# Two block plans in turn, and layer 0's maxima on another engine, in a fused two-layer graph-attention kernel

## The chip, the core and the metric

The kernel runs on one core of a Trainium2 chip. The core has five engines, each with a queue of its own that is worked off in order: TensorE (PE: matrix products into PSUM; its weight loads are PEld), VectorE (DVE), ScalarE (ACT), GpSimd (POOL, which does not read PSUM here) and SyncE (SP, which issues nearly all DMAs of this kernel). The metric is the device time of one execution in microseconds (us).

## The reference

Two layers over a graph of 3327 nodes with 128 features; `adj` is 3327 x 3327, 0 or 1, with ones on the diagonal.

```python
# layer 0: x = layernorm(x + gat(x, adj))
Hm = X @ W.T + b;  s = Hm @ a_s;  r = Hm @ a_r
e = leaky_relu(A * s + A * r.T, 0.2)
att = softmax(where(A > 0, e, NEG), axis=1);  out = att @ Hm
# layer 1: x = layernorm(x + graphormer(x, adj, adj)), H = 8
q, k, v = ((x @ Wq.T).reshape(d, n, h), ...)
a = einsum('dnh,dmh->dnm', q, k) * d ** -0.5
a = softmax(a + adj + adj, axis=2)
out = einsum('dnm,dmh->dnh', a, v).reshape(n, h * d) @ Wo.T
```

Layer 1 is the work: for each of the 128 features a full 3327 x 3327 attention with head size 8.

## The kernel before, in words

**Tiles.** The features are taken in 32 *groups* of 4. The 3327 queries are cut into 7 *blocks* of 476 (the last 472), so there are 224 blocks. The 3327 keys are 26 *chunks* of 128 or 127. For a block and a chunk the kernel needs scores (keys x queries) for 4 features, the exponential of twice (score/2 + adj), and the product with the values, which is summed over the 26 chunks in one PSUM tile `av`.

**Scores** (`pair_scores`, L154): two matmuls of one pair of features make one PSUM tile `scb` of 2 x 476 columns. A chunk has two halves (h = 0, 1), one for each pair.

**Two ways to bring in the adjacency.** Most chunks: VectorE adds `adj` to the PSUM scores and writes SBUF (L1139), half by half, and ScalarE later takes the exponential in SBUF (`exp_late`, L968), a whole chunk of 1904 columns at a time. GpSimd's chunks (`times`: 0, 3, ..., 24): ScalarE takes the exponential straight out of PSUM (L1136), and GpSimd multiplies by a factor that is 1 or e squared (L1137). The factor is made from `adj` by GpSimd (`make_factor`, L782) the first time and kept in DRAM (`ftd`). In what follows P is an exponential out of PSUM (952 columns), S a whole one in SBUF (1904 columns).

**Rounds.** A block is 26 *rounds* of two halves. Of three chunks i, i+1, i+2 the rounds are A: (i, half 1) and (i+1, half 0); B: (i, half 0) and (i+1, half 1); C: both halves of i+2. So A and B have one add and one P each, C two adds. Each round issues in this order: the loads of a coming stretch, the four score matmuls, the P and its multiplication or the adds, the S that have fallen due (`late`, normally the round after the chunk's last add), the products of the chunk that stands four rounds back (`products`, L938; LAG = 4), and side work. Chunks 24 and 25 are the last two rounds (A and B alone). Chunk 23's and chunk 25's exponentials are not done whole: `late` lists their halves one by one, chunk 23's in the last two rounds, chunk 25's in the first two rounds of the next block.

**Buffers.** `scb` has one PSUM tile for the chunks of `times` (pool `pe`) and two for the others (pool `pd`); `av` has one: the first products of a block wait until VectorE has copied the block before out of it (`o4`, L948, issued just behind the last products, which come in the fourth round of the next block). The exponentials have 7 tiles (`e4`), the loaded adjacency 5 (`at`, one for each *stretch* of three chunks; `want_adj` asks for it AHEAD = 3 stretches early). Side work has one PSUM tile (`bank`).

**Side work.** Layer 0 for rows of 128 queries, the projections to q, k, v that follow it, and the output projection of finished rows run in the gaps. They are lists of units: kind "p" for TensorE, "d" for VectorE, "m" for GpSimd, "x" for DMAs. `lane` says in which rounds a unit may be issued (mostly the B rounds), `work_tensor` and `work` issue them. Layer 0's weights are `weigh` (a maximum of a row and a scalar, L310, 650 of them on VectorE) and `mask` (times `adj`, GpSimd, L319). A projection is cut in columns of 128 (`QW`): `project` (TensorE), then `halves` on VectorE: the rounded value `hi` (L405) and the remainder `lo` (L408). `finish_to` forces what is not done when the keys of the next group are loaded. `judge` tests at the end that the shortcuts were valid for the data (if not, a slower general program runs, which is not the case here).

Of the kernel before, what the change touches and what calls it, by code (L numbers as in the profile page):

```python
# [8 lines left out]
F32 = mybir.dt.float32  # L9
# [8 lines left out]
P = 128  # L18
# [29 lines left out]
def kernel(  # L48
# [70 lines left out]
    NTR = NT // 3  # L119
    NP = NTR + (NT % 3 == 2)  # L120
    times = {3 * j for j in range(NP)}
    stretch = [list(range(i, min(i + 3, NT))) for i in range(0, NT, 3)]
    NST = len(stretch)
    where = {i: (i % 3 if NT % 3 != 1 or i < NT - 1 else 1) for i in range(NT)}
    assert all(kr[i] == P for i in times)
# [26 lines left out]
    def special():  # L152
# [9 lines left out]
        with ExitStack() as sx, tc.manual_schedule(engines=ALL):  # L162
# [106 lines left out]
            def layer0(t, side=True, trow=None, bank=bank, held=None):  # L269
# [31 lines left out]
                def weigh(n, c0, c1):  # L301
# [3 lines left out]
                    for i in range(c0, c1):  # L305
                        w, e = s["w"][n][:, i - i0, :r], er[:, i : i + 1]
                        if side:

                            w = s["w"][n][:, i - i0, :].rearrange("p (a b) -> p a b", b=T3)
                            nc.vector.tensor_scalar(w, s["t"][:, :, :T3], e, None, op0=ALU.max)  # L310
# [79 lines left out]
                QW = 128 if side else 512  # L390
# [7 lines left out]
                def halves(dst, c, scale):  # L398
# [3 lines left out]
                    o = c % 512  # L402
                    hi, lo = s["hi"], s["lo"]
                    if side:
                        nc.vector.tensor_scalar(hi[:r, o : o + QW], s["b"][:r, :QW], scale, None, op0=ALU.mult)  # L405
                    else:
                        nc.scalar.mul(hi[:r, o : o + QW], s["b"][:r, :QW], scale)
                    nc.vector.scalar_tensor_tensor(  # L408
# [34 lines left out]
                for w, dst, sc in ((wk, kT, 1.0), (wq, qT, half_scale)):  # L443
                    for c in range(0, H * D, QW):
                        chain += [
                            ("p", lambda w=w, c=c: project(w, c)),
                            ("d", lambda dst=dst, c=c, sc=sc: halves(dst, c, sc)),
# [15 lines left out]
                for n, (i0, i1) in enumerate(CH):  # L463

                    aside.append(("n", ("P", q0 + n - 2, 0)))
                    for c0 in range(i0, i1, 3):
                        c1 = min(c0 + 3, i1)
                        aside.append(("d", lambda n=n, c0=c0, c1=min(c0 + 2, c1): weigh(n, c0, c1)))
                        if c0 + 2 < c1:
                            aside.append(("d", lambda n=n, c0=c0 + 2, c1=c1: weigh(n, c0, c1)))  # L470
                        if side:
                            aside.append(("m", lambda n=n, c0=c0, c1=c1: mask(n, c0, c1)))
# [269 lines left out]
            stretches = [(g, b, m) for g in range(NG) for b in range(NBLK) for m in range(NST)]  # L742
            adjs = {}
            RAW = max(NBLK, AHEAD + 3) * NST

            def want_adj(n):
# [6 lines left out]
                cs = stretch[m]  # L753
                if n >= RAW and cs[0] in times:
                    nc.sync.dma_start(a[:, 0, :w], ftd[b][m][:, :w])
                    cs = cs[1:]
                for of in [cs[:-2], cs[-2:]] if len(cs) > 2 else [cs]:
                    if not of:
                        continue
                    z = where[of[0]]  # L760
# [16 lines left out]
            def make_factor(n):  # L777
                if n < min(RAW, len(stretches)) and stretch[stretches[n][2]][0] in times:
                    g, b, m = stretches[n]
                    w = exact[b][2]  # L780
                    f = adjs[n][:, 0, :w]
                    nc.gpsimd.tensor_scalar(f, f, E2 - 1.0, 1.0, op0=ALU.mult, op1=ALU.add)  # L782
                    if g == 0:
                        issue(lambda: nc.sync.dma_start(ftd[b][m][:, :w], f))
# [132 lines left out]
            rounds, order, starts = [], [], {}  # L917
            for m, st_ in enumerate(stretch):
                starts[len(rounds)] = m
                if len(st_) > 1:  # L920
                    i = st_[0]
                    rounds += [[(i, 1), (i + 1, 0)], [(i, 0), (i + 1, 1)]]
                    order += [i + 1, i]
                for i in st_[2:] if len(st_) > 1 else st_:
                    rounds.append([(i, 0), (i, 1)])
                    order.append(i)
            NR = len(rounds)
# [56 lines left out]
            def lane(kind, n):  # L984
                middle = n % 3 == 1 and 4 <= n < NR - 2
# [558 lines left out]
```

## Time and profile before

| what | value |
|---|---|
| median of three runs | 10001.89 us (9998.2 to 10005.2) |
| profiled execution | 10004.91 us |
| its span (first to last instruction) | 10003.1 us |
| granted TensorE clock | 0.996 |
| P: L1136 on ScalarE | 4032, mean 1012 ns |
| S and halves: L968 on ScalarE | 4256, mean 1678 ns |
| adds: L1139 on VectorE | 7616, mean 1143 ns |
| multiplications: L1137 on GpSimd | 4032, mean 2237 ns |
| DMA | 1728.31 MB, mean 173 GB/s |

Busy time is the union of an engine's instructions; their mean durations can overlap, so the time that one more instruction costs is read from start to start. A row of a group has count, busy us, mean ns of one, then the idle time before them and what ended it. A row of a timeline has the start (us from the span's start), the duration, engine, line, operation, tiles, shape and count; in brackets the idle time of the engine before it and what ended that.

### The profile page before, as it was taken

How to read it: one execution, taken by the hardware profiler on the slowest of the kernel's cores; microseconds unless marked ns; L12 is line 12 of the kernel's file. 1: busy time of each engine (PE TensorE's matmuls, PEld its weight loads, DVE VectorE, ACT ScalarE, POOL GpSimd, SP SyncE). 2: the span in 40 equal slices, each digit the busy share in tenths (PEclk: the TensorE clock that was granted, in tenths of full speed). 3: DMA queues.
4: the chain of work that ended last, by engine and by line, in shares of the span. 5: the costliest groups of instructions: out<-in, count | busy, mean ns of one | idle time of the engine just before them, and what ended most of it. 6: DMA issues, size and time to landing. Idle time of an engine off the chain costs nothing.

```text
span 10003.1 us, 212173 instructions
## 1 busy us (share of the span) xinstructions
PE 9461.4 (95%) x81923; PEld 3078.5 (31%) x81923; DVE 9334.1 (93%) x11592; ACT 9892.4 (99%) x8352; POOL 9201.7 (92%) x4416
## 2 busy tenths in 40 slices
PE   7999999999999999999999999999999999999998
PEld 2233333333233333323333332333332333332222
DVE  7999999999999999999999999999999999999998
ACT  7999999999999999999999999999999999999998
POOL 7999999999999999999999999999999999999998
PEclk9999999999999999999999999999999999999999
DMA  7665666655656656656566665566665566656554
GB/s 200 200 176 169 177 172 177 178 167 174 177 165 175 182 161 178 177 169 176 165 173 174 181 179 164 163 178 179 177 174 168 164 179 177 175 161 171 167 168 125
DMA packets 1383200, 1728.31 MB, mean 173 GB/s; under 512 B 347463, under 2 KB 1370657, under 8 KB 1378079
## 3 DMA queue, kind: packets, MB, share of 16 engines
q1 hardware_dynamic: 1371828, 1712.03, 60.1%
q8 instruction: 644, 10.55, 0.4%
q10 hardware_dynamic: 10347, 2.61, 0.1%
q14 instruction: 381, 3.12, 0.1%
HBM read 1610.23 MB, written 103.93 MB: 171 GB/s over the span
## 4 chain that ended last, share of the span: by engine, by line
ACT 40%; PE 24%; POOL 16%; issue 11%; DVE 6%; DMA 2%; SPq 1%; POOLq 0%; ACTq 0%; DVEq 0%
ACT e L968 25%; POOL e L1137 16%; ACT e L1136 15%; PE scb L154 12%; PE av L938 11%; DVE e L1139 4%; PE bank L243 1%; DVE o L948 1%; DVE lo L408 0%; DMA q4b<-qT 0%; POOL w L319 0%; DMA at<-ftd 0%; DVE hi L405 0%; DMA k4b<-kT 0%; DVE w L310 0%
## 5 line engine op out<-in xcount | busy, mean ns | idle before, releaser
L1137 POOL TENSOR_TENSOR e<-e,at 128x952 f32<-128x952 f32 (+1 forms) x4032 | 8956.7, 2237 | 718.9 <-ACT e L1136 641.7
L1139 DVE TENSOR_TENSOR e<-scb,at 128x952 f32<-128x952 f32 (+1 forms) x7616 | 8420.0, 1143 | 579.3 <-PE scb L154 477.8
L968 ACT ACTIVATE e<-e 128x1904 f32<-128x1904 f32 (+2 forms) x4256 | 7104.0, 1678 | 2.0 <-DVE e L1139 1.6
L938 PE MATMUL av<-e,v4b 128*32 128x476 f32 x46592 | 5917.6, 572 | 60.6 <-DVE o L948 41.9
L154 PE MATMUL scb<-q4b,k4b 32*128 32x476 f32 (+1 forms) x23296 | 3749.2, 486 | 442.8 <-ACT e L1136 370.8
L1136 ACT ACTIVATE e<-scb 128x952 f32<-128x952 f32 (+1 forms) x4032 | 4078.6, 1012 | 57.5 <-PE scb L154 33.8
L154 PEld LDWEIGHTS scb<-q4b,k4b 32*128 32x128 f32 (+1 forms) x23296 | 1764.2, 189 | 5371.8 <-ACT e L1136 3489.9
L938 PEld LDWEIGHTS av<-e,v4b 128*32 128x32 f32 x46592 | 1059.2, 108 | 1140.0 <-issue 933.0
L243 PE MATMUL bank<-hsb,w 128*32 128x129 f32 (+1 forms) x5200 | 277.8, 285 | 0.0
L328 DVE TENSOR_SCALAR_CACHE_REDUCE dump<-a 128x384 bf16<-128x384 f32 (+2 forms) x468 | 247.1, 528 | 0.6
L319 POOL TENSOR_TENSOR w<-w,a 128x384 f32<-128x384 f32 (+3 forms) x225 | 207.7, 923 | 0.1
L310 DVE TENSOR_SCALAR w<-trow,er 128x129 f32<-128x129 f32 x650 | 201.1, 338 | 0.0
L948 DVE COPY o<-av 128x476 f32<-128x476 f32 (+1 forms) x224 | 145.9, 651 | 8.1 <-PE av L938 7.2
L243 PEld LDWEIGHTS bank<-hsb,w 128*32 128x32 f32 (+1 forms) x5200 | 102.4, 108 | 148.0 <-issue 148.0
L408 DVE SCALAR_TENSOR_TENSOR lo<-bank,hi 128x128 fp32r<-128x128 f32 (+1 forms) x400 | 116.5, 291 | 13.8
L405 DVE TENSOR_SCALAR hi<-bank 128x128 fp32r<-128x128 f32 (+1 forms) x400 | 112.0, 280 | 0.0
L243 PE MATMUL bank<-wv,x1T 128*32 128x128 f32 x1600 | 85.6, 286 | 3.9 <-DVE vb L429 3.9
L243 PE MATMUL bank<-wq,x1T 128*32 128x128 f32 x1600 | 85.4, 285 | 0.0
L243 PE MATMUL bank<-wk,x1T 128*32 128x128 f32 x1600 | 85.4, 285 | 0.0
L243 PE MATMUL bank<-wo,ot 128*32 128x128 f32 x1600 | 85.2, 285 | 0.0
L429 DVE COPY vb<-bank 128x128 f32<-128x128 f32 (+1 forms) x200 | 56.1, 281 | 5.8 <-PE bank L243 5.8
L503 PE MATMUL bank<-ident,o 128*128 128x128 f32 x225 | 52.0, 304 | 0.0
(123 smaller groups left out, 659.7 us busy)
## 6 DMA issues: line engine op xcount, KB each, us to landing
at<-in_adjT_dram SPq DMA_DIRECT2D x1536, 476.0 KB
at<-ftd SPq DMA_DIRECT2D x1674, 238.0 KB
at<-in_adjT_dram SPq DMA_DIRECT2D x256, 472.0 KB
at<-ftd SPq DMA_DIRECT2D x279, 236.0 KB
k4b<-kT SPq DMA_DIRECT2D x128, 415.9 KB
q4b<-qT SPq DMA_DIRECT2D x1528, 29.8 KB
at<-in_adjT_dram SPq DMA_DIRECT2D x186, 208.2 KB
a<-in_adjT_dram SPq DMA_DIRECT2D x50, 504.0 KB
```

The source lines that it names most:

```text
L154: nc.tensor.matmul(dst, k4[32 * j : 32 * j + H4, first_key(i) : first_key(i) + 2 * r - 1 : 2], q4[32 * j : 32 * j + H4, :nb], start=True, ...
L243: nc.tensor.matmul(dst[c0:c1], w[:, c0:c1], mov, **kw)
L310: nc.vector.tensor_scalar(w, s["t"][:, :, :T3], e, None, op0=ALU.max)
L319: nc.gpsimd.tensor_tensor(w, w, s["a"][n][:, c0 - i0 : c1 - i0, :r], op=ALU.mult)
L328: nc.vector.tensor_scalar(z, a, float(k), None, op0=ALU.is_equal, op1=ALU.add, accum_out=even[:, t, at : at + 1])
L408: nc.vector.scalar_tensor_tensor(lo[:r, o : o + QW], s["b"][:r, :QW], scale, hi[:r, o : o + QW].bitcast(F32), op0=ALU.mult, op1=ALU.subtract,)
L938: nc.tensor.matmul(s.av[32 * j : 32 * j + 32, : s.w], s.v4[:r, j, i * H1 : i * H1 + 32], e[:r, j, : s.w], start=(s.left == NT - 1), stop=( ...
L948: nc.vector.tensor_copy(o4[:, :w], s.av[:, :w])
L968: nc.scalar.activation(e, e, AF.Exp, scale=2.0)
L1136: nc.scalar.activation(eh, z[:r, :, :w], AF.Exp, scale=2.0)
L1137: nc.gpsimd.tensor_tensor(eh, eh, ah, op=ALU.mult)
L1139: nc.vector.tensor_tensor(eh, z[:r, :, :w], ah, op=ALU.add)
```

## The change

- **Two plans in turn.** Even blocks (counted over the whole run) keep 9 chunks for GpSimd. An odd block starts with a round of chunk 25 alone (two adds), goes on with the eight triples, and ends with one round of chunk 24 alone: its half 1 goes the GpSimd way, its half 0 is added by VectorE. So an odd block has 17 P and 35 adds in place of 18 and 34. It has ten stretches in place of nine, and chunk 24 needs both its factor and its plain adjacency there.
- **Exponentials whole.** `late` no longer splits chunks 23 and 25; all are due one round after the last add. The one half left is chunk 24's in odd blocks.
- **Maxima on GpSimd.** `weigh` becomes a GpSimd `tensor_scalar` (minimum with 3e38, then maximum), three to a unit of kind "m", and `mask` is a unit of its own.
- **Projections of 256 columns** in place of 128, and `halves` becomes `high` (kind "d") and `low` (kind "l"), which is issued a round after.
- **Other places for side work.** `lane` depends on the plan: in odd blocks all places are one round later, and "m" units, which had one in any round, now go only where "d" units may. Even: rounds 4, 7, ..., 22, 0 and 25; odd: 5, 8, ..., 23 and 25; "l" one round after each. "p" has also the round 3 (odd: 4).
- **Factors.** `made_by` holds the stretch that makes a block's factor, since the two plans number their stretches differently.

```diff
+    threes = [(i, [i + 1, i + 2]) for i in range(0, NT - 2, 3)]
+    plans = [threes + [(NT - 2, [NT - 1])], [(None, [NT - 1])] + threes + [(NT - 2, [NT - 2])]]
...
-                            nc.vector.tensor_scalar(w, s["t"][:, :, :T3], e, None, op0=ALU.max)
+                            nc.gpsimd.tensor_scalar(w, s["t"][:, :, :T3], -LOWEST, e, op0=ALU.min, op1=ALU.max)
...
-                QW = 128 if side else 512
+                QW = 256 if side else 512
...
-                            ("d", lambda dst=dst, c=c, sc=sc: halves(dst, c, sc)),
+                            ("d", lambda c=c, sc=sc: high(c, sc)),
+                            ("l", lambda dst=dst, c=c, sc=sc: low(dst, c, sc)),
...
-                        aside.append(("d", lambda n=n, c0=c0, c1=min(c0 + 2, c1): weigh(n, c0, c1)))
-                        if c0 + 2 < c1:
-                            aside.append(("d", lambda n=n, c0=c0 + 2, c1=c1: weigh(n, c0, c1)))
-                        if side:
-                            aside.append(("m", lambda n=n, c0=c0, c1=c1: mask(n, c0, c1)))
+                        aside.append(("m", lambda n=n, c0=c0, c1=c1: weigh(n, c0, c1)))
+                        aside.append(("m", lambda n=n, c0=c0, c1=c1: mask(n, c0, c1)))
...
+            def kind(g, b):
+                return (g * NBLK + b) % 2
...
+                times, adds = plans[kind(g, b)][m]
+                at = int(times is not None)
+                runs = [(at, adds)]
+                if times is not None:
+                    if made_by.setdefault((b, times), n) < n:
+                        nc.sync.dma_start(a[:, 0, :w], ftd[b][times // 3][:, :w])
...
+            def laid(plan):
+                rounds, order, starts = [], [], {}
+                for m, (i, adds) in enumerate(plan):
+                    starts[len(rounds)] = m
+                    if i is None:
+                        rounds += [[(k, 0, n), (k, 1, n)] for n, k in enumerate(adds)]
+                        order += adds
+                    elif i in adds:
+                        rounds.append([(i, 1, None), (i, 0, 1)])
+                        order.append(i)
+                    else:
+                        rounds += [[(i, 1, None), (adds[0], 0, 1)], [(i, 0, None), (adds[0], 1, 1)]]
+                        rounds += [[(k, 0, n + 1), (k, 1, n + 1)] for n, k in enumerate(adds) if n]
+                        order += [adds[0], i] + adds[1:]
+                return rounds, order, starts
...
-            def lane(kind, n):
-                middle = n % 3 == 1 and 4 <= n < NR - 2
-                if kind == "p":
-                    return int(middle or n == 3 or n >= NR - 2)
-                return int(middle or n == 0 or n >= NR - 2)
+            def reading(n, odd):
+                n -= odd
+                if n % 3 == 1 and 4 <= n < NR - 2:
+                    return True
+                return n in ((NR - 2,) if odd else (0, NR - 1))
+
+            def lane(kind, n, odd):
+                if kind == "l":
+                    return int(reading(n - 1, odd) if n else True)
+                return int(reading(n, odd) or kind == "p" and n - odd == 3)
...
-                        for i, h in rnd:
-                            if i in times:
-                                continue
-                            if NT % 3 == 2 and i == NT - 1:
-                                late.append((now + 2, s, i, 2 * h, 2 * h + 2))
-                            elif NT % 3 == 2 and i == NT - 3:
-                                late.append((now + 1 + h, s, i, 2 * h, 2 * h + 2))
-                            elif added[i] == 2 and (now + 1, s, i, 0, HG) not in late:
-                                late.append((now + 1, s, i, 0, HG))
+                        for i in [i for i, hs in added.items() if len(hs) == 2 or odd and i == NT - 2]:
+                            hs = added.pop(i)
+                            late.append((now + 1, s, i, 2 * min(hs), 2 * max(hs) + 2))
```

## The prediction

> **What bounds the kernel now.** I read the page first, then the groups kept apart by shape, then the timeline of single instructions where one block passes into the next and inside a block, then the busy times by stretch.
>
> ```profile
> PE 9461.4 (95%) x81923; PEld 3078.5 (31%) x81923; DVE 9334.1 (93%) x11592; ACT 9892.4 (99%) x8352; POOL 9201.7 (92%) x4416
> ```
>
> ScalarE is busy for 99% of the span: it is the bound, and three others are close behind it. So what counts is how long ScalarE's slots are and when it waits. The groups by shape (count, busy us, mean ns):
>
> ```profile
> L968 ACT ACTIVATE e<-e 128x1904 f32<-128x1904 f32 x2880 | 5299.5, 1840 | 1.0 <-DVE e L1139 0.9
> L968 ACT ACTIVATE e<-e 128x952 f32<-128x952 f32 x384 | 425.0, 1107 | 0.0
> L782 POOL TENSOR_SCALAR at<-at 128x476 f32<-128x476 f32 x54 | 32.0, 592 | 4.6
> masks.py:199 POOL TENSOR_SCALAR_AFFINE_SELECT ident<-ident 128x128 f32<-128x128 f32 x1 | 0.3, 297 | 0.0
> ```
>
> The means overlap each other, so a slot is read from one start to the next. ScalarE alone, where one block passes into the next (start, duration):
>
> ```profile
> 4545.93 1.06 ACT L1136 ACTIVATE e<-scb 128x952 f32<-128x952 f32 x1
> 4546.77 1.10 ACT L968 ACTIVATE e<-e 128x952 f32<-128x952 f32 x1
> 4547.66 1.07 ACT L1136 ACTIVATE e<-scb 128x952 f32<-128x952 f32 x1
> ...
> 4549.43 1.04 ACT L1136 ACTIVATE e<-scb 128x952 f32<-128x952 f32 x1
> ...
> 4551.18 1.03 ACT L1136 ACTIVATE e<-scb 128x952 f32<-128x952 f32 x1
> ...
> 4554.66 0.96 ACT L1136 ACTIVATE e<-scb 128x952 f32<-128x952 f32 x1
> ```
>
> An exponential out of PSUM (P) takes a slot of 0.84, a half one in SBUF 0.89. A whole one (S) takes 1.68, as two P + S pairs last 5.05 (9289.99 to 9295.04, two P starts of the window below). The half slots are the chunks 23 and 25, which ScalarE takes in two pieces; a pair of halves costs 0.10 more than one whole.
>
> TensorE, VectorE just after that place:
>
> ```profile
> 4551.89 0.91 PE L154 MATMUL scb<-q4b,k4b 32*128 32x476 f32 x4
> ...
> 4552.72 1.42 PE L938 MATMUL av<-e,v4b 127*32 127x476 f32 x8
> ...
> 4554.07 0.50 PE L154 MATMUL scb<-q4b,k4b 32*128 32x476 f32 x4
> ...
> 4555.79 0.65 DVE L948 COPY o<-av 128x476 f32<-128x476 f32 x1
> ...
> 4556.50 0.16 PEld L938 LDWEIGHTS av<-e,v4b 128*32 128x32 f32 x8 [0.23 <-DVE o L948]
> ```
>
> Here TensorE stands still until VectorE has copied the block's output out of PSUM. In the middle of a block, where nothing of that happens:
>
> ```profile
> 9289.99 1.02 ACT L1136 ACTIVATE e<-scb 128x952 f32<-128x952 f32 x1
> ...
> 9293.02 3.26 DVE L1139 TENSOR_TENSOR e<-scb,at 128x952 f32<-128x952 f32 x3 [0.24 <-PE scb L154]
> ...
> 9294.18 0.53 PE L154 MATMUL scb<-q4b,k4b 32*128 32x476 f32 x4
> 9294.64 1.00 PE L938 MATMUL av<-e,v4b 128*32 128x476 f32 x8
> 9295.04 1.03 ACT L1136 ACTIVATE e<-scb 128x952 f32<-128x952 f32 x1
> ...
> 9296.12 0.50 PE L154 MATMUL scb<-q4b,k4b 32*128 32x476 f32 x4 [0.48 <-ACT e L1136]
> ...
> 9296.69 1.15 DVE L1139 TENSOR_TENSOR e<-scb,at 128x952 f32<-128x952 f32 x1 [0.41 <-PE scb L154]
> ```
>
> Three adds run on end: two of a round with two adds (call it C), one of the next (A). TensorE's B round at 9296.12 waited for ScalarE. Stretches (us; busy of PE, PEld, DVE, ACT, POOL; clock, DMA): an ordinary block, and one in which five projections are forced through at once:
>
> ```profile
> 4551.18:4595.29 44.11, 42.22 (x364) 13.46 (x360) 42.19 (x59) 44.11 (x39) 42.64 (x22) 1.00 0.61 179
> 668.64:717.19 48.55, 45.18 (x428) 15.02 (x424) 42.88 (x57) 44.11 (x38) 40.29 (x21) 0.96 0.80 198
> ```
>
> **The change part by part.** The sum is made against the profiled execution, 10004.91 us (span 10003.1), which is 3.0 above the median of the three runs.
>
> *ScalarE's slots: less.* Two blocks now hold 36 P, 30 S, 8 halves: 36 x 0.844 + 30 x 1.681 + 8 x 0.887 = 87.9; measured 2 x 44.11 = 88.22, so 0.31 are waits or pace. After: 35 P, 34 S, one half = 34 x 2.525 + 0.84 + 0.89 = 87.58. Of the 0.31, 0.09 lies in the stretch worked out next; the rest goes with P's duration, which creeps from 0.96 to 1.07 within a block and falls back at each boundary, and I keep 0.13 of it (bounds 0 and 0.22).
>
> *Odd into even block: a new wait.* After the change only one half, that of chunk 24, lies between the first P of the even block and its fourth. TensorE's side: the P at 4549.43 ends 1.04 later; the PSUM buffer of GpSimd's chunks is single, so the next scores start at 4550.52, the following ones at 4551.89, their products at 4552.72. These took 1.42, waiting for the late half of chunk 25; without that 0.94, so the fourth round's scores start at 4553.66 and the P follows 0.59 later (4554.07 to 4554.66), at 4554.25: 4.82 after the first. ScalarE's own slots in it are 0.84 + 0.89 + 0.84 + 1.68 = 4.25. It waits 0.57. (Now they are 5.14, and 5.23 are measured.)
>
> *Even into odd block: a new wait.* The odd block opens with chunk 25, a round of two adds, so the block's order is shifted by one round and the copy of the output (L948) comes behind the two adds of a C round instead of one of an A round. In the window above it would stand at 9293.02 + 2 x 1.06 = 9295.14 and end at 9295.79. Queued behind it are A's add and TensorE's products, which start at 9295.85 instead of 9294.64; B's scores move from 9296.12 to 9296.79; its add to 9297.36, ending 9298.51. The S that needs it was due at 9295.04 + 2.53 + 0.84 = 9298.41 and starts at 9298.57. The second pair of the next scores waits for the same buffer: 9298.56, products 0.42 later, next A scores 9299.92, P 9300.51 where 9300.09 was due. ScalarE waits 0.42.
>
> Two blocks: 87.58 + 0.13 + 0.57 + 0.42 = 88.70 against 88.22; + 0.48 x 112 = +54. Bounds: the waits 0 and 1.3 (side work in the way), so -57 to +90.
>
> *Forced projections: gone.* The changed order has none. Blocks 6 and 13 each held five (48.55 against 44.11): -9 (0 to -10).
>
> *Judge* (range tests) moves from the last group to group 27, with three rounds instead of two before its first matmul. ScalarE's 3.8 wait at 9879.8 for TensorE, which waited for GpSimd's squares, and 1.4 in the block after go, unless they only move: -5 (0 to -6).
>
> *Maxima on GpSimd*: 650 instructions leave VectorE (338 ns) and one multiplication of 2.19 leaves GpSimd in each odd block. No row shows the new form. Below it is 0.16 (592 ns scaled by 129/476), above 0.59 (the same operation at nearly four times the width); I take 0.30 from the 128-wide one-input row. GpSimd in the worst two blocks: 35 x 2.19 + 18 x 0.30 + 6 x 0.92 (L319) = 87.6 of 88.7, and a chunk's products start 2.5 us after its multiplication ends (9290.79 to 9293.25), so lateness is covered: 0. At 0.59 it is 92.8, 4.1 over the 88.7 and 1.6 more than that cover; with the burst of each row's last third two to four us a row, 25 rows, +50 to +100. In the first seven blocks GpSimd also makes 63 factors (0.66 each) and is the bound (the first three take 145.3 for 54 multiplications, 28 factors and 9 masks, 145.1): one multiplication less there, 26 maxima more, then two less and nine more: +4 (-5 to +15).
>
> The Trainium skill (GPSIMD Engine Reference, When to use GPSIMD) names VectorE for elementwise max and calls GpSimd's one-input operations roughly line rate. By its per-element figure (1.03 cycles at 1.2 GHz, section Performance versus the Vector engine) I estimate 0.11 us for 129 columns before dispatch; no row here shows that. By it GpSimd would never be late and the sum would not change, and against the rule's choice of engine the trace says that neither engine is the bound.
>
> *Hidden at zero:* 112 more adds (1.06) on VectorE, which loses 650 maxima and half of 600 projection pieces (280 to 291 ns) and has about 0.8 free in each three rounds (5.05 less four adds); if that cover goes, the S that follows has 0.57 left (an add ends at 9292.78, its S starts at 9293.35). The 256-wide projections take some 0.2 more of TensorE in a B round, whose next P has 0.3 left. On SP's queue one more load of 238 KB in each odd block, 27 of 1728 MB, and the lead of a tile falls from 11 rounds to 9, about 15 us. The split-off remainder (`l`) stands in the round after and delays A's add by 0.3, within B's slack.
>
> Sum: 54 - 9 - 5 + 4 = +44: 10049.
>
> **The rivals.**
> 1. *The boundary waits are hidden.* Were VectorE or TensorE ahead of these rows at the boundaries, only the slots would show: (87.71 - 88.22) x 112 - 10 = -67: 9938, faster. Place: the fourth P of an even, the seventh round of an odd block. It decides once both waits come to less than 0.42 per two blocks. For it: 0.3 to 1.0 of slack lies before each P in a block. Against: the PSUM chain above is already without slack.
> 2. *One boundary waits, the other not* (the copy gets in between the two adds' ends, say): 0.06 x 112 - 10 = -3: 10002, no change.
> 3. *GpSimd becomes the bound* in the rows' bursts: from 0.47 us a maximum on, at 0.59 about +75 more: 10110.
>
> **How the numbers follow.** Forecast 0.52 (10049; its own range 10020 to 10080, from keeping 0 or 0.22 of the pace, and 0.2 on each wait); rival 1 0.15, rival 2 0.17, rival 3 0.16. The range 9985 to 10105 leaves out rival 1 and a third of rival 3. About 0.2%, 20 us, can be told from no change: slower is the forecast and rival 3 (0.68), the same rival 2 (0.17), faster rival 1 (0.15).
>
> **What would show it.** Two blocks together at 88.7 instead of 88.2; ScalarE's P waiting for TensorE's scores about 0.5 once near the start of each block and nowhere else; the output copy starting 1 us after the products' end in odd blocks only; blocks 6 and 13 ordinary; a 128x129 row on GpSimd near 0.30. Wrong would be: P starts 2.5 apart across both boundaries, or TensorE's products waiting for GpSimd.

## The result and the profile after

| | before | after |
|---|---|---|
| median, runs beside each other | 10002.3 us (9998.2 to 10006.5, 6 runs) | 10067.9 us (10065.7 to 10070.1, 6 runs) |
| profiled execution | 10004.91 us | 10067.05 us |
| its span | 10003.1 us | 10065.3 us |
| start of the last P to the end of the span | 29.0 us | 29.2 us |

The ratio is 1.0065, 95% interval 1.0053 to 1.0078: slower by 65 us. The forecast was 10049 (9985 to 10105), slower.

The first part of the page of after:

```profile
PE 9418.8 (94%) x79523; PEld 2994.8 (30%) x79523; DVE 9195.1 (91%) x10554; ACT 9914.3 (99%) x7904; POOL 9185.0 (91%) x4954
```

ScalarE is still the bound. It has 448 instructions fewer than before (8352) and its busy time is 22 us longer all the same, because the recorded durations overlap: busy time would have misled here, and slots from start to start do not. The groups of after, kept apart by shape (count | busy us, mean ns of one | idle time before):

```profile
L986 ACT ACTIVATE e<-e 128x1904 f32<-128x1904 f32 x3072 | 5617.6, 1829 | 16.2 <-DVE e L1167 3.5
...
L308 POOL TENSOR_SCALAR w<-trow,er 128x129 f32<-128x129 f32 x650 | 233.6, 381 | 1.3
...
L986 ACT ACTIVATE e<-e 128x952 f32<-128x952 f32 x96 | 104.4, 1088 | 0.0
```

The 384 half exponentials are down to 96, and a maximum on GpSimd takes 381 ns.

**Odd into even block.** Timeline of after, the last P of odd block 99 is just before; the first line is the first P of even block 100 (L1164 is P, L986 is S, L152 scores, L956 products):

```profile
4534.98 1.02 ACT L1164 ACTIVATE e<-scb 128x952 f32<-128x952 f32 x1
4535.82 1.07 ACT L986 ACTIVATE e<-e 128x952 f32<-128x952 f32 x1
...
4536.05 0.49 PE L152 MATMUL scb<-q4b,k4b 32*128 32x476 f32 x4 [0.70 <-ACT e L1164]
...
4536.70 1.04 ACT L1164 ACTIVATE e<-scb 128x952 f32<-128x952 f32 x1
...
4537.41 0.91 PE L152 MATMUL scb<-q4b,k4b 32*128 32x476 f32 x4
...
4537.87 1.79 ACT L986 ACTIVATE e<-e 128x1904 f32<-128x1904 f32 x1
...
4538.25 1.00 PE L956 MATMUL av<-e,v4b 128*32 128x476 f32 x8
...
4539.19 0.51 PE L152 MATMUL scb<-q4b,k4b 32*128 32x476 f32 x4
...
4539.77 0.96 ACT L1164 ACTIVATE e<-scb 128x952 f32<-128x952 f32 x1
```

The half of chunk 24 at 4535.82 is the only exponential between the first two P. From the first P to the third, at 4539.77, pass 4.79 us, and ScalarE has 4.25 of slots for them.

**Even into odd block.** Timeline of after, fourth round of odd block 101 and what follows (L966 is the output copy, L1167 an add):

```profile
4583.36 2.21 DVE L1167 TENSOR_TENSOR e<-scb,at 128x952 f32<-128x952 f32 x2 [0.24 <-PE scb L152]
4583.60 1.00 PE L956 MATMUL av<-e,v4b 128*32 128x476 f32 x8
...
4585.33 1.08 ACT L1164 ACTIVATE e<-scb 128x952 f32<-128x952 f32 x1
4585.49 0.64 DVE L966 COPY o<-av 128x476 f32<-128x476 f32 x1
...
4586.19 1.00 PE L956 MATMUL av<-e,v4b 127*32 127x476 f32 x8 [1.12 <-DVE o L966]
...
4587.70 1.15 DVE L1167 TENSOR_TENSOR e<-scb,at 128x952 f32<-128x952 f32 x1 [0.51 <-PE scb L152]
4587.85 1.09 ACT L1164 ACTIVATE e<-scb 128x952 f32<-128x952 f32 x1
...
4588.94 1.79 ACT L986 ACTIVATE e<-e 128x1904 f32<-128x1904 f32 x1
...
4590.26 0.81 PE L152 MATMUL scb<-q4b,k4b 32*128 32x476 f32 x4
...
4590.85 0.96 ACT L1164 ACTIVATE e<-scb 128x952 f32<-128x952 f32 x1
```

The products before the copy end at 4584.60; the copy stands behind two adds and starts 0.89 later, TensorE stands still for 1.12, S starts at 4588.94 where 4588.69 was due, and the next P at 4590.85, 3.00 after the one before it instead of 2.53.

Windows of after (length, then busy us of PE, PEld, DVE, ACT, POOL): blocks 100 and 101 and block 6, and then blocks 92 and 93, which carry 11 maxima:

```profile
4534.98:4580.28 45.30, 43.07 (x371) 13.90 (x367) 40.81 (x49) 45.06 (x38) 40.21 (x19) 1.00 0.50 150
4580.28:4623.69 43.41, 40.75 (x364) 13.49 (x364) 38.58 (x40) 43.30 (x35) 38.01 (x18) 1.00 0.54 159
355.10:406.30 51.20, 43.20 (x324) 11.65 (x324) 41.68 (x48) 45.74 (x38) 49.28 (x41) 0.93 0.85 222
```

```profile
4180.20:4268.97 88.77, 84.14 (x735) 27.43 (x728) 82.00 (x102) 88.41 (x72) 86.95 (x54) 1.00 0.55 161
```

An even and an odd block together take 88.71; the median over the run is 88.75 (before: 88.22). Block 6 is bound by GpSimd (49.28 of 51.20).

**Where the 62.1 us between the two profiled executions lie.** Blocks are set against each other by the starts of chunk 12's first P.

| place | us |
|---|---|
| two waits in each of 112 pairs of blocks, 88.75 - 88.22 | +59.4 |
| forced projections of blocks 6 and 13, gone | -9.0 |
| GpSimd in the first 14 blocks (+0.4 in all, less -9.0 and 7 x 0.53) | +5.7 |
| range tests: +4.9 around blocks 191 to 193, -6.6 in the last two blocks | -1.7 |
| one late load at block 77 | +3.2 |
| spread over the rest | +4.5 |

The -9.0 is read from block 13 alone (48.56 before against an ordinary 44.11, and 43.05 after). For block 6, which GpSimd bounds after the change, the same is assumed, and what is left of the first 14 blocks is put down to GpSimd.

### The profile page after: what moved, and what is told of

Its sections match the earlier page's. It is cut to its first block, busy times and chain, and to the rows that moved or that the text cites. A ratio compares the mean times of both kernels' runs of the same rounds, so it can differ in the third digit from the quotient of the medians.

```text
span 10065.3 us, 207546 instructions
## 1 busy us (share of the span) xinstructions
PE 9418.8 (94%) x79523; PEld 2994.8 (30%) x79523; DVE 9195.1 (91%) x10554; ACT 9914.3 (99%) x7904; POOL 9185.0 (91%) x4954
## 5 line engine op out<-in xcount | busy, mean ns | idle before, releaser
L1165 POOL TENSOR_TENSOR e<-e,at 128x952 f32<-128x952 f32 (+1 forms) x3920 | 8723.4, 2238 | 793.4 <-ACT e L1164 737.1
L1167 DVE TENSOR_TENSOR e<-scb,at 128x952 f32<-128x952 f32 (+1 forms) x7728 | 8507.2, 1143 | 801.9 <-PE scb L152 682.1
L986 ACT ACTIVATE e<-e 128x1904 f32<-128x1904 f32 (+3 forms) x3920 | 7088.8, 1808 | 20.1 <-DVE e L1167 5.1
L956 PE MATMUL av<-e,v4b 128*32 128x476 f32 (+1 forms) x46592 | 5839.8, 573 | 162.7 <-DVE o L966 133.9
L152 PE MATMUL scb<-q4b,k4b 32*128 32x476 f32 (+1 forms) x23296 | 3816.0, 486 | 448.7 <-ACT e L1164 381.4
L1164 ACT ACTIVATE e<-scb 128x952 f32<-128x952 f32 (+1 forms) x3920 | 3932.0, 1003 | 76.9 <-PE scb L152 30.0
L152 PEld LDWEIGHTS scb<-q4b,k4b 32*128 32x128 f32 (+1 forms) x23296 | 1763.5, 189 | 5418.3 <-ACT e L1164 3159.6
L956 PEld LDWEIGHTS av<-e,v4b 128*32 128x32 f32 (+1 forms) x46592 | 1010.7, 108 | 1312.6 <-issue 940.5
L241 PE MATMUL bank<-hsb,w 128*32 128x129 f32 (+1 forms) x5200 | 278.3, 286 | 0.0
L308 POOL TENSOR_SCALAR w<-trow,er 128x129 f32<-128x129 f32 x650 | 233.6, 381 | 1.3
L966 DVE COPY o<-av 128x476 f32<-128x476 f32 (+1 forms) x224 | 144.2, 644 | 5.2 <-PE av L956 5.2
L241 PEld LDWEIGHTS bank<-hsb,w 128*32 128x32 f32 (+1 forms) x5200 | 102.5, 108 | 148.4 <-issue 148.4
L241 PE MATMUL bank<-wo,ot 128*32 128x128 f32 x1600 | 85.2, 285 | 0.0
L409 DVE SCALAR_TENSOR_TENSOR lo<-bank,hi 128x256 fp32r<-128x256 f32 (+1 forms) x200 | 83.0, 415 | 0.0
L402 DVE TENSOR_SCALAR hi<-bank 128x256 fp32r<-128x256 f32 (+1 forms) x200 | 83.0, 415 | 0.0
L241 PE MATMUL bank<-wv,x1T 128*32 128x256 f32 x800 | 63.9, 391 | 0.0
L241 PE MATMUL bank<-wq,x1T 128*32 128x256 f32 x800 | 63.9, 391 | 0.0
L241 PE MATMUL bank<-wk,x1T 128*32 128x256 f32 x800 | 63.9, 391 | 0.0
```

Of the source, the lines that this page charges most:

```text
L152: nc.tensor.matmul(dst, k4[32 * j : 32 * j + H4, first_key(i) : first_key(i) + 2 * r - 1 : 2], q4[32 * j : 32 * j + H4, :nb], start=True, ...
L241: nc.tensor.matmul(dst[c0:c1], w[:, c0:c1], mov, **kw)
L308: nc.gpsimd.tensor_scalar(w, s["t"][:, :, :T3], -LOWEST, e, op0=ALU.min, op1=ALU.max)
L956: nc.tensor.matmul(s.av[32 * j : 32 * j + 32, : s.w], s.v4[:r, j, i * H1 : i * H1 + 32], e[:r, j, : s.w], start=(s.left == NT - 1), stop=( ...
L966: nc.vector.tensor_copy(o4[:, :w], s.av[:, :w])
L986: nc.scalar.activation(e, e, AF.Exp, scale=2.0)
```

## The experiments

Four sets of runs, each beside runs of the kernel before on the same chip (medians 10002.8, 10001.7, 10006.0, 10001.9; so a difference between two sets is uncertain by some 4 us).

**1. Put a half slot back into the first place.**

```diff
                         for i in [i for i, hs in added.items() if len(hs) == 2 or odd and i == NT - 2]:
                             hs = added.pop(i)
+                            if odd and i == NT - 3:
+                                late += [(now + 1, s, i, 0, 2), (now + 2, s, i, 2, HG)]
+                                continue
```

> The changed kernel (10067.9 us), but in odd blocks chunk 23's exponential is split again: one half due in the round after its last add, the other in the first round of the even block. Theory (odd into even: too few ScalarE slots lie between the first and the fourth P of the even block, 4.25 us against a TensorE and PSUM chain of 4.82): with one more half slot of 0.89 in that stretch it holds 5.14, so the wait of 0.57 goes, for 0.10 of splitting: -0.47 in each of 112 pairs of blocks, -53 us: about 10015, and the second gap between P starts of an even block about 3.4 instead of 3.10 with ordinary 2.5 behind it. Rival (TensorE or VectorE is late there through side work or GpSimd, so that the P waits whatever ScalarE holds): the wait stays and the split is paid: 10068 to 10080.

10021.6 us (11 runs; ratio to before 1.0020, 1.0010 to 1.0029): 46 less. Timeline of ScalarE in this run, the same place:

```profile
4518.62 1.03 ACT L1164 ACTIVATE e<-scb 128x952 f32<-128x952 f32 x1
4519.48 1.94 ACT L986 ACTIVATE e<-e 128x952 f32<-128x952 f32 x2
4521.25 1.02 ACT L1164 ACTIVATE e<-scb 128x952 f32<-128x952 f32 x1
4522.10 1.86 ACT L986 ACTIVATE e<-e 128x1904 f32<-128x1904 f32 x1
4523.78 1.03 ACT L1164 ACTIVATE e<-scb 128x952 f32<-128x952 f32 x1
```

P, two halves, P, S, P: 5.16 from the first P to the third, all of it ScalarE's own slots. The expected second gap of 3.4 isn't there: the gaps are 2.63 and 2.53, since the second half stands between the first two P and not behind the second; the sum of the two is the one expected. The pair is at 88.28, 0.47 less. The other wait is untouched (3.02). So the first wait comes from too little work for ScalarE between these P. That side work is not its cause is shown by two runs below: with the old side work (plans alone) and with the maxima on VectorE, the same gap has the same median, 3.09.

**2. Copy between the two adds.**

```diff
-                                nc.vector.tensor_tensor(eh, z[:r, :, :w], ah, op=ALU.add)
+                                add = lambda eh=eh, z=z, r=r, ah=ah: nc.vector.tensor_tensor(eh, z[:r, :, :w], ah, op=ALU.add)
+                                if odd and n == 3 and h == 1:
+                                    last_add.append(add)
+                                else:
+                                    add()
...
+                        while last_add:
+                            last_add.pop()()
```

The last two lines stand behind the products, and so behind the copy.

> The changed kernel, but in odd blocks the output copy is issued between the two adds of its round in place of behind both. Theory (even into odd: the copy stands behind two adds, so products, the next scores and the add behind them are late): the copy comes about 1 us earlier for the products, the second add 0.65 later; the wait of 0.47 in each odd block shrinks to 0.2 to 0.25: -20 to -30 us: 10038 to 10048. Rival (the copy's place is not the cause; the shifted order of the loads and the side work is): unchanged, 10068.

10049.3 us (ratio to before 1.0045, 1.0032 to 1.0059): 19 less, a little short of the 20 to 30 expected. ScalarE in this run, odd block 101:

```profile
4576.56 1.08 ACT L1164 ACTIVATE e<-scb 128x952 f32<-128x952 f32 x1
4577.71 1.79 ACT L986 ACTIVATE e<-e 128x1904 f32<-128x1904 f32 x1
4579.41 0.94 ACT L1164 ACTIVATE e<-scb 128x952 f32<-128x952 f32 x1
```

The P that was late is on time (its gap is 2.52 in the median, 2.99 after). But the wait has moved one place forward and shrunk from 0.47 to 0.32: S, due at 4577.40, now starts 0.31 late. This S needs the add that was put behind the copy. So the copy's place held up that P; with the copy moved, the next in line is that add.

**3 and 4. Side work alone, and plans alone.** The third run puts only the side work of the change (maxima on GpSimd, 256 columns, remainder a round later, new places) on the plans of before; the other keeps only plans and whole exponentials.

Side part alone, on the kernel before (of its edit, the unit lists, `high` and `low`, and `lane` are those of the change and not shown):

```diff
-                            nc.vector.tensor_scalar(w, s["t"][:, :, :T3], e, None, op0=ALU.max)
+                            nc.gpsimd.tensor_scalar(w, s["t"][:, :, :T3], -LOWEST, e, op0=ALU.min, op1=ALU.max)
...
-                QW = 128 if side else 512
+                QW = 256 if side else 512
...
-                        work(g * total + at, n)
+                        work(g * total + at, n, 0)
```

> The kernel before (10002.3 us) with the side work of the change alone: maxima on GpSimd, projections of 256 columns with the remainder one round later, the new places; one plan for all blocks and the split exponentials as before. Theory (the two plans cost the time, at the two boundaries): the forced projections gone (-9), GpSimd slower in the first seven blocks (+5 to +10), so 9998 to 10008: the same as before. Rival (GpSimd's maxima or the new places cost the time): 10040 to 10070.

Plans alone, on the kernel after (the same parts put back to those of before, not shown):

```diff
-                            nc.gpsimd.tensor_scalar(w, s["t"][:, :, :T3], -LOWEST, e, op0=ALU.min, op1=ALU.max)
+                            nc.vector.tensor_scalar(w, s["t"][:, :, :T3], e, None, op0=ALU.max)
...
-                QW = 256 if side else 512
+                QW = 128 if side else 512
...
-                        work(g * total + at, n, odd)
+                        work(g * total + at, n - odd)
```

> The changed kernel's block plans and whole exponentials with the side work of before: maxima on VectorE two or one at a time, projections of 128 columns, places of before counted from the block's first triple. Theory (the boundaries cost 0.53 in each pair of blocks whatever the side work does): +59, and up to +30 where VectorE, with one more add in each odd block, is late with its 650 maxima: 10058 to 10092. Rival (the side work that alone cost 45 us costs the same in the changed kernel, and the plans only the remaining 20): 10015 to 10030.

| | time | last P starts at | from there to the end |
|---|---|---|---|
| before (profiled) | 10004.9 | 9974.1 | 29.0 |
| side part alone (profiled; median 10048.2) | 10051.5 | 10020.4 | 29.3 |
| plans alone (profiled; median 10157.8) | 10162.1 | 10037.2 | 123.1 |
| after (profiled) | 10067.1 | 10036.1 | 29.2 |

Both expectations failed, and for the same reason: the parts aren't independent. Up to the last P the plans cost 63 with the old side work and 62 with the new, as the two boundaries said. But with the old side work 94 us more lie behind the last P. And the new side work, which up to there costs nothing on the new plans, costs 46 on the old ones. Experiments 5 to 7 take these two surprises apart.

**5. Side part alone, maxima back on VectorE.** One line of the run before, `nc.gpsimd.tensor_scalar(w, ...)`, becomes `nc.vector.tensor_scalar(w, ..., op0=ALU.max)`.

> The side part alone on the plans of before (measured: +45 us), but with layer 0's maxima on VectorE in the same places. Theory (with nine chunks in every block GpSimd has no room for the maxima: 36 multiplications of 2.19, 18 maxima of 0.38 and 6 masks of 0.92 are 91.2 us in two blocks of 88.2): nearly all of the 45 goes, and 5 to 10 more where GpSimd bounds the first blocks: 9988 to 10008. Rival (the 256-wide projections or the new places cost the time): 10030 to 10050.

10016.5 us (ratio 1.0015, 1.0005 to 1.0024): 32 of the 45 go. In the waits of the run with maxima on GpSimd (engine, tile, line, what it waited for: us in all, times, longest):

```profile
PEld av L939 <- POOL e L1148: 205.4, 444, 4.1
...
PE av L939 <- POOL e L1148: 91.4, 138, 3.8
```

TensorE's weight loads and products wait for GpSimd's multiplications, 297 us in the two rows together (they can overlap); before it is 57, with the maxima on VectorE 105. By count, a unit of three maxima (1.14) and two multiplications (4.48) need 5.6 us in three rounds that last 5.05, so GpSimd falls behind with each unit and has to catch up. At the boundary of two blocks the plans of before leave it no gap for that: the multiplications of four P follow each other there, and the one of a block's second P ends 4.75 us after this P starts (median of blocks 16 to 187; 3.83 in even blocks after the change, some 3.3 in the middle of a block).

The trace of the side part alone shows where the time goes. In blocks 16 to 187 the gap from a block's fourth P to its fifth is 2.53 us in the 112 blocks with no GpSimd side work around the boundary, and 3.31 in the 26 with most of it (some 3 us). This one place holds 26 of the 39 us that these blocks take more than before. With the maxima on VectorE the mean gap at this place is 2.52 again (2.68 with them on GpSimd). Half of what the move gains in the profiled runs (16.7 of 33 us up to the last block) lies in the first 14 blocks, where GpSimd also makes the factors. With the maxima on VectorE the first 14 blocks are 5.9 faster than before, and 25 us come back up to block 182; these weren't taken apart.

**6. Projections of 128 columns in the changed kernel.**

```diff
-                QW = 256 if side else 512
+                QW = 128 if side else 512
```

> The changed kernel with projections of 128 columns again (their remainder still a round later): 12 more units in each of 25 rows, in the places that two block plans offer. Theory (the width is what lets the side work fit: the plans alone left 123 us after the last P, where the changed kernel leaves 29): the body stays at the changed kernel's length (last P 10030 to 10045) and the range tests and output projections slip to the end: 10090 to 10170. Rival (the places suffice; the tail of the plans alone came from maxima that shared the VectorE places): no tail, 10062 to 10075.

10207.4 us, more than expected. The body is as long as expected (last P at 10045.0), but 157.6 us follow it. ScalarE's last exponentials and the first output transfer behind them (issued on its queue), and below the waits after that point:

```profile
10044.97 1.04 ACT L1164 ACTIVATE e<-scb 128x944 f32<-128x944 f32 x1
10045.80 2.75 ACT L986 ACTIVATE e<-e 128x1888 f32<-128x1888 f32 x2
10179.59 0.74 ACTq L970 DMA_DIRECT2D oT<-o  x2
```

```profile
POOL ot L621 <- PE bank L241: 106.7, 1, 106.7
...
PE bank L502 <- DMA o<-oT: 52.7, 6, 8.9
```

The range tests (L621) start only when output projections (L241) that no round had a place for are done. In plans alone the same line reads 71.2 us. So the width of 256 hardly changes the loop (9 us): it is what lets the side work end inside the loop, now that there are fewer places (for VectorE's units 10 in every block before, 9 and 8 by turns after). It is also what removes the forced projections: in this run they are back, and blocks 6 and 13 take 54.07 and 59.98 us (51.19 and 43.05 in after).

**7. Maxima away from GpSimd, and twice on it, in the changed kernel.**

```diff
-                            nc.gpsimd.tensor_scalar(w, s["t"][:, :, :T3], -LOWEST, e, op0=ALU.min, op1=ALU.max)
+                            nc.vector.tensor_scalar(w, s["t"][:, :, :T3], e, None, op0=ALU.max)
```

and, in the other run, the GpSimd line twice.

> The changed kernel, but layer 0's maxima run on VectorE again, in the same places. Theory (GpSimd bounds only the first seven blocks; elsewhere the 381 ns of a maximum are hidden): -6 to -12 us, all of it in the first seven blocks: 10056 to 10062. Rival (GpSimd is the bound in the bursts of each row's last third): -30 to -60: 10010 to 10040. VectorE late instead (650 maxima of 338 ns back on an engine that has less free time than before): +10 to +30.

> The changed kernel with each of layer 0's 650 maxima issued twice on GpSimd (the second writes the same values again): 650 x 0.36 = 234 us more of GpSimd. Forecast's view (hidden until a maximum costs about 0.47 us; twice is 0.72, over that): +50 to +100 in the rows' bursts and about +9 in the first seven blocks: 10120 to 10180. If GpSimd has more slack than that count gave it: 10068 to 10090. If it were already the bound in the changed kernel (every added us shows): 10250 to 10300.

On VectorE: 10080.0 us, 12 more than the changed kernel; the first 14 blocks take 11.8 less, as expected, and then each 14 blocks 2 more, 27 in all, so that the third possibility is the one that came. Twice on GpSimd: 10334.3 us, 266 more by the medians (259 by the ratios to before) for 242 us of added work; of the expectations the one for an engine that is already the bound is nearest. Pairs of blocks 16 to 181, by the number of maxima of one kind that fall into them:

| maxima in the pair | after: pairs, mean us | twice: pairs, mean us (maxima counted double) |
|---|---|---|
| 0 to 5 | 33, 88.84 | 24, 88.87 |
| 6 to 11 | 36, 88.69 | 16, 90.67 |
| 12 to 17 | 14, 88.64 | 2, 91.63 |
| 18 to 23 | | 21, 92.09 |
| 24 to 29 | | 15, 94.57 |
| 30 to 35 | | 5, 94.79 |

In the changed kernel a pair with maxima is no longer than one without: they are hidden. The second set costs all it takes: a straight line through the pairs of the other run gives 0.37 us for each maximum added. Windows of this run: blocks 92 and 93, with 28 of them, and 100 and 101, with none:

```profile
4315.94:4414.40 98.46, 88.60 (x736) 27.49 (x728) 82.42 (x102) 88.85 (x71) 93.50 (x72) 0.93 0.49 145
```

```profile
4683.45:4728.76 45.31, 43.08 (x372) 13.90 (x368) 40.80 (x49) 45.07 (x37) 40.22 (x19) 1.00 0.50 151
4728.76:4772.17 43.41, 40.74 (x364) 13.51 (x364) 38.56 (x40) 43.29 (x35) 37.97 (x18) 1.00 0.54 161
```

GpSimd is busy for only 95% of the long pair: it isn't full over two blocks. By the count of experiment 5 it is late in the rounds that have a unit.

**8. The even plan in every block.**

```diff
-                return (g * NBLK + b) % 2
+                return 0
```

> The changed kernel with the even plan in every block: nine chunks for GpSimd, whole exponentials, no odd plan. Theory (what the order puts between two P that share one PSUM buffer decides): at each boundary the P of chunk 24's second half and of chunk 0's first follow each other with no S between, so that gap is 1.73 (as the trace of before has it) in place of a slot of 0.844; a block is 18 x 0.844 + 17 x 1.681 + 0.89 = 44.66, 0.28 more than the changed kernel's 44.38: +63, about 10130; GpSimd, with 36 multiplications in two blocks, may add up to 30: 10120 to 10160. Rival (the whole exponentials save their 0.10 and the gap is hidden): 43.77 to 43.9 a block, 9930 to 9960.

10157.4 us, at the upper end of the theory's range; a block takes 44.73 in the median, 44.66 by the theory. ScalarE in this run, from one block into the next:

```profile
4580.29 1.09 ACT L1164 ACTIVATE e<-scb 128x952 f32<-128x952 f32 x1
4582.09 0.96 ACT L1164 ACTIVATE e<-scb 128x952 f32<-128x952 f32 x1 [0.71 <-PE scb L152]
```

The gap from the last P of a block to the first of the next is 1.80 here and 1.76 to 1.79 over the run, where ScalarE's slot is 0.84: two P one after the other, with no S between, wait for the one PSUM tile. So with whole exponentials the even plan alone costs 90 us more than the two plans in turn.

**9. Towards a faster version.** Experiments 1 and 2 together; then with the maxima of seven rows on VectorE and a longer wait in the range tests; then with the late S behind the copy in two halves.

```diff
+                            if t <= 7:
+                                nc.vector.tensor_scalar(w, s["t"][:, :, :T3], e, None, op0=ALU.max)
...
-                            ("w", 2),
+                            ("w", 6),
...
+                            if odd and n == 3:
+                                late += [(now + 1, s, i, 0, 2), (now + 1, s, i, 2, HG)]
+                                continue
```

> The changed kernel with both edits: chunk 23's exponential split in odd blocks (measured alone: 10021.6) and the output copy between the two adds (alone: 10049.3). Theory (two separate waits, 14 us apart, each with its own cause): the gains of 46 and 19 add up, 10003 (9999 to 10008). Rival (the waits were also the cover of GpSimd and VectorE, which are late next): half of the smaller gain or less, 10010 to 10022.

> The two edits of the run before this one, and two more: the maxima of the first seven rows (blocks 0 to 14) run on VectorE, where GpSimd makes the factors and is the bound, and the range tests' totals wait six rounds for GpSimd's squares in place of two. Theory: 11 less in the first fourteen blocks (with all rows on VectorE they took 11.8 less) and 3 to 5 less at the range tests: 14 to 16 under the run before, about 9988 if that one is at 10003. Rival (lateness moves on to VectorE): the same as the run before.

> The last run (halves, copy between the adds, first rows' maxima on VectorE: 9995.5) with one more edit: in odd blocks the exponential of the chunk whose second add now stands behind the output copy is issued as two halves one after the other. In the trace of that last run this exponential starts 0.40 after ScalarE is free (4552.66, where the P before it began at 4551.42 and takes a slot of 0.84), because the second add ends only at 4552.5. Theory (that add is all it waits for): the first half starts 0.40 earlier, splitting costs 0.10: -0.3 in each of 112 pairs, about 9962. Rival (the scores and adds behind the copy are late as well): the P or S after it takes the wait over, 9988 to 9996.

The first: 10005.7 us (ratio 1.0002, 0.9993 to 1.0011), within the theory's 9999 to 10008: the gains add up, the two waits are separate. The second: 9995.5 us (0.9992, 0.9983 to 1.0001), 10 less where 14 to 16 were expected. The first 14 blocks gave 12.8; the tests gave 1 at most; and the seven rows reach to block 44 and not, as the expectation has it, to 14: between blocks 14 and 42 this run gave 3.4 back. The third: 9985.4 us beside 10006.0 (0.9979, 0.9970 to 0.9988): faster than both kernels, by 0.2%, but of the 33 us expected of the last edit only some 13 came (by the two ratios). ScalarE in that run, odd block 101:

```profile
4549.99 1.18 ACT L1167 ACTIVATE e<-scb 128x952 f32<-128x952 f32 x1
4550.84 2.11 ACT L989 ACTIVATE e<-e 128x952 f32<-128x952 f32 x2
4552.61 1.19 ACT L1167 ACTIVATE e<-scb 128x952 f32<-128x952 f32 x1
4553.45 2.03 ACT L989 ACTIVATE e<-e 128x1904 f32<-128x1904 f32 x1
4555.27 1.06 ACT L1167 ACTIVATE e<-scb 128x952 f32<-128x952 f32 x1
```

The halves start on time (4549.99 + 0.85). But the P at 4555.27 comes 1.82 after the S before it, whose slot is 1.68: its scores are late, as the rival had it. The gaps are 2.62 and 2.66 where the run before has 2.94 and 2.53.

## Why the prediction was right, and which terms were off

**Sign, bound and mechanism: right.** Slots from start to start gave 87.58 for a pair; with the 0.13 kept and both waits 88.70 was forecast and 88.75 measured.

- *Odd into even, 0.57:* measured 0.57 (median gap 3.09 less 2.52). The chain was foretold to the step: scores 1.09 and 2.46 after the first P, products at 3.29, P at 4.82; after shows 1.07, 2.43, 3.27 and 4.79. Experiment 1 removes it with nothing but ScalarE work moved into the gap, and experiment 8 makes such a wait by taking the work out of another boundary. The text called the late P the fourth; it is the third P of the block, in its fourth round. The Trainium skill (Perfetto Trace Analysis, Identifying Performance Opportunities) says that the same gap repeated on the engine that should be saturated can mean that a tile lacks buffers; this case agrees as to the cause, with P's single PSUM tile and experiments 1 and 8, but shows another cure than a buffer: work for the engine in between. No run here gave P a second tile.
- *Even into odd, 0.42:* measured 0.47. The copy started 0.89 after the products' end (1 us foretold), S was 0.25 late (0.16), P 0.48 (0.42). Both together: +59.4 in place of +54; the term was undersized by 5.
- *The 0.13 of pace:* the sum is right, its reason isn't. It was put down to P's duration creeping up within a block. In experiment 1 the duration creeps on through the boundary (1.00 at 4509.31, 1.14 at 4559.12) with slots unchanged; the 0.13 of after are small leftovers right behind the two waits (gaps of 2.54 to 2.60).
- *Forced projections, -9:* gone as foretold; block 13 takes 43.05. But it is the width of 256 that removes them (experiment 6), which the prediction put at zero, and block 6 wasn't ordinary: GpSimd made it 51.2 long.
- *Judge, -5:* wrong, -1.7 measured. The step was "go, unless they only move": they moved, and cost 4.9 at their new place. Timeline of after while the tests run:

```profile
8636.51 0.97 ACT L1164 ACTIVATE e<-scb 128x952 f32<-128x952 f32 x1 [0.33 <-PE scb L152]
...
8647.17 0.97 ACT L1164 ACTIVATE e<-scb 128x952 f32<-128x952 f32 x1 [0.33 <-PE scb L152]
...
8671.50 1.84 DVE L638 TENSOR_TENSOR jz<-jz,jy 128x1 f32<-128x1 f32 x1
...
8675.55 1.79 ACT L986 ACTIVATE e<-e 128x1904 f32<-128x1904 f32 x1 [1.66 <-DVE e L1167]
...
8680.70 0.96 ACT L1164 ACTIVATE e<-scb 128x952 f32<-128x952 f32 x1 [0.82 <-PE scb L152]
```

  Ahead of the first, a square on GpSimd runs from 8631.68 to 8632.74, TensorE's total starts at 8632.80 after 0.29 of waiting for it, and VectorE's reduction of the total (0.68) holds up the add and so the scores. The three rounds that were to cover the square did not. The larger part is not behind a square: one small test on VectorE (L638) takes 1.84 us where the same line took 0.16 at 8660.71, the adds behind it come late, and S and the next P wait 1.66 and 0.82. Why it takes so long is open. It takes 0.16 in the run of experiment 2, where 2.6 of the 19 us gained lie here, and in the first run of experiment 9, where this stretch is 3 us shorter than in after. That left little for a longer wait for the squares to gain.
- *Maxima, 0.30 each and hidden, +4:* 0.381 each, hidden from block 16 on by the table of experiment 7, +5.7 in the first 14 blocks. The 0.11 before dispatch that I had estimated from the Trainium skill's per-element figure (GPSIMD Engine Reference, Performance versus the Vector engine) is under a third of the measured 0.381. Its rule that VectorE is the engine for an elementwise maximum (When to use GPSIMD) agrees with the first 14 blocks (11.8 less with VectorE), and not with the others (27 more).
- *"27 of 1728 MB" more on SP's queue, hidden:* except once. At block 77 VectorE's adds wait 2.2 us for an adjacency tile, from the waits of after between 3513 and 3530:

```profile
DVE e L1167 <- DMA at<-in_adjT_dram: 2.2, 2, 1.6
```

- *256 columns at zero:* right for the time they add. That the new plans need them, for 139 us (experiment 6), the prediction did not see: it counted what each unit costs and not how many places are left.
- *Products waiting for GpSimd*, which the prediction named as a sign that it would be wrong, did come: 134 us in TensorE's two rows of after, 57 before. Of these, 72 (before 47) lie in the first 700 us. From there to 8500 us they are 55 (before 7), none longer than 0.7, and the table of experiment 7 shows that ScalarE doesn't lose by them.

**The rivals.** That the boundary waits are hidden, or one of them, is out by the gaps. Rival 3, GpSimd as the bound, didn't come about at 0.381. But its price was far too small: "at 0.59 about +75 more" came from GpSimd's busy time over two blocks, less a cover of 2.5. (Its figures also don't meet: by its own terms the threshold of 0.47 would be 0.50, and 10049 + 75 is 10124 and not 10110.) At twice 0.37 the added cost is some 260. By count, lateness arises in the three rounds that have a unit (4.48 + 2.28 = 6.8 against 5.05); experiment 3 shows it at 0.38 with one multiplication more. Where exactly between 0.38 and 0.74 the cover ends in the changed kernel wasn't measured.

The sum was +44 and is +62.1 between the profiled executions: +5 from the two waits, +3 from the judge, +2 from the first blocks, +3 from the late load, +4.5 not assigned.

## What to carry to other kernels

On an engine that is full, count its slots between two instructions that share one PSUM tile, and set them against the chain from the first through the other engines to the second: an edit that saves instructions there can cost more than it saves, and moving half an instruction back into the stretch brought four times its price (46 us for 0.10 x 112). Count an engine's load over the rounds in which a unit of side work stands and not over a long stretch, and count the places that side work has left, for what doesn't fit turns up behind the loop. Before judging one part of a change by itself, try both parts alone: here one alone costs 45, the other 156, and both 65.

## What the runs showed of the hardware that was not expected

- ScalarE's recorded durations grow while it never waits: in the last version P's go from 1.03 at 4499.40 to 1.19 at 4552.61, and back to 1.06 behind the next wait, while the slots stay at 0.84 and 1.68. The recorded duration isn't the price of an instruction.
- A GpSimd maximum of 128x129 takes 381 ns and the factor of 128x476 (L793, of the same operation) 591 ns: from these two I estimate some 300 ns for any such instruction and 0.6 ns for an element in each partition, if the two differ in nothing but their size.
- The work added on GpSimd in experiment 7 came back at about its full length (266 us by the medians, 259 by the ratios, for 242), though GpSimd was busy for only 91% of the span.
